# Summing half one's x1 + lam·y early on POOL, output stores on POOL's queue with more tiles, and the transform stored in loading order

## Chip, cores, metric

One core of one Trainium2 chip. Times are device microseconds of one execution on that core. "Engine" means PE (matrix multiply), DVE (vector), ACT (activation), POOL (GpSimd) or SP, which here does nothing but issue transfers: all the loads, so that I call its queue the loading queue, and some stores. A "queue" is the series of transfers that one of these engines issues, in its own program order. All runs in this text are of the fast state, with a mean granted PE clock between 0.907 and 0.925.

## The reference, cut to what matters

Two layers on an image of 256 channels of 256x128. The change touches only the end of the second. In the reference:

```python
attn = instance_norm(attn + tokens, attn_norm_w, attn_norm_b)
attn = attn.reshape(b * (C // TOKEN_CODIM), TOKEN_CODIM, H, W)
h0 = instance_norm(attn, norm2_w, norm2_b)
h1 = fno_layer(h0, mix_wr[0], ..., (H, W), norm=True, act=True)   # Gelu
h2 = fno_layer(h1, mix_wr[1], ..., (H, W), norm=True)
out = instance_norm(h2, mon_w, mon_b) + attn
# and around it:  x = x + layer(_gn(x))
```

In the kernel's names: `x1` is the image after layer one, `y` the attention output before its norm, `lam` a factor per channel. The last line is, per pixel, `x1 + lam*y + kap*h2 + c0`. `x1 + lam*y` does not depend on h1 or h2, so it can be had as soon as `lam` is known. The 256 channels are two halves (a = 0, 1) of 128 partitions; a half is 16 blocks of 2048 pixels (NB), 1 MB each in f32.

## The kernel before

```python
# stage A: y of both halves, 16 blocks each
    ...
    nc.scalar.dma_start(ydv[:, a, b * NB : (b + 1) * NB], yt)
# stage B: first_modes, end
    for a, h in enumerate(halves):
        synth_modes(wp, pss, Z[:, :, :, a * P : (a + 1) * P], P, h.Gd1, f"g1{a}", turned=True)

def first_images(a, beside=None):
    def begin(b):
        if a == 0 and b >= 4:
            yt = hb[b]                      # y is still in SBUF
        else:
            yt = wp.tile([P, NB], FP, tag="yt", ...)
            nc.sync.dma_start(yt, ydv[:, a, b * NB : (b + 1) * NB])
        ...                                 # PE: skip and image into ps
        for j in range(4):
            nc.scalar.activation(by_turn(hb[b])[:, j], ps[j]..., AF.Gelu)
    for b in range(17):
        if b < 16:
            if beside is not None:
                beside(b, op, psk)          # second_images(0, b)
            begin(b)
        if b > 0:
            ...                             # transposes hT, statistics, psA of block b - 1
            nc.scalar.copy(yA, psA)
            nc.scalar.dma_start(h.Yd[:, b - 1, :], yA)

def second_modes(a):
    ...   # YT <- Yd: sixteen loads; norm z; synthesis g2a

def second_images(a, b, wp, psk):
    for s in range(2):
        yt.append(wp.tile([P, half], FP, tag="yo", ..., bufs=2))
        nc.sync.dma_start(yt[s], ydv[:, a, px])
        xt.append(wp.tile([P, half], FP, tag="xo", ..., bufs=3))
        nc.sync.dma_start(xt[s], x1v[:, a, px])
    ...                                     # PE, then ACT Identity into hb[b]
    for s in range(2):
        nc.vector.scalar_tensor_tensor(xt[s], yt[s], lam, xt[s], ALU.mult, ALU.add)
        nc.vector.tensor_tensor(xt[s], xt[s], hb[b][...], ALU.add)
        nc.scalar.dma_start(outv[:, a, px], xt[s])

first_modes()                                            # B
first_images(0)                                          # C
second_modes(0)                                          # D
first_images(1, beside=... second_images(0, b, ...))     # E
second_modes(1)                                          # F
for b in range(16): second_images(1, b, wp, psk)         # G
```

`yA` (128x512) is the transform of one block. The pace of the yA copies is the pace of the blocks, and it serves as the clock of stages C and E in everything below.

## Time and profile before

3370.2 us median of four runs (3364.2 to 3379.4); the profiled run's span is 3364.9 us. The prediction names seven stages, A to G, and shows a table of them with rounded borders. For exact lengths I take as borders instructions that the loading queue issues in every variant: the first y load of C, the load of the transform that begins D and F, the first x or y load of E and G. B is counted from 2479.4 us, where A ends in before. A's last addition ends somewhat later in most other runs (2480.2 us in after, 2488.6 at the latest), and this difference, which belongs to what comes before B, is then in B's length too.

| stage | what it does | us | bound, as the prediction reads it |
|---|---|---|---|
| B | first modes, both halves | 103.7 | serial |
| C | first images of half one | 141.5 | PE |
| D | second modes of half one | 76.4 | serial |
| E | first images of half two, second images of half one | 285.8 | transfers |
| F | second modes of half two | 77.1 | serial |
| G | second images of half two | 201.0 | transfers and tiles |

Two more views matter later. The first is ACT's timeline of before in C: start, duration, instruction, and in brackets the idle time ahead of it and what ended it.

```profile
2627.68 0.58 ACT L1221 COPY yA<-psA 128x512 f32<-128x512 f32 x1 [3.25 <-PE psA L1217]
...
2629.82 2.06 ACT L1168 ACTIVATE blocks<-ups 128x512 f32<-128x512 f32 x4 [1.56 <-PE ups L949]
2631.74 0.62 ACT L1181 COPY hT<-htps 128x512 f32<-128x512 f32 x1
2635.61 0.58 ACT L1221 COPY yA<-psA 128x512 f32<-128x512 f32 x1 [3.25 <-PE psA L1217]
```

One block takes 2635.61 - 2627.68 = 7.93 us. ACT works 0.58 + 2.06 + 0.62 us of it and otherwise waits for PE. There is room for more on ACT, provided it stands in ACT's order where the gaps are.

The second is the loading queue's own waits in E (total us, times, longest).

```profile
SPq L1306 <- DMA out_dram<-x: 84.5, 27, 7.3
SPq L1304 <- DVE x L1319: 35.0, 21, 3.0
```

The queue stands 120 of E's 286 us for xo and yo tiles to come free.

### The profile page before, as it was taken

The page shows a single profiled execution, that of the slowest core. Times are in us where ns is not written, and L with a number is a line of the kernel's source. Part 1 is how long each engine was busy: PE and PEld are TensorE (multiplying, and loading weights), DVE is VectorE, ACT ScalarE, POOL GpSimd, SP SyncE. Part 2 cuts the span into 40 slices and gives each one's busy share as a digit, 9 for nine tenths or more (in the row PEclk, how much of TensorE's full clock was granted, in tenths as well). Part 3 has the DMA queues.
Part 4 walks back from the last instruction along what each step waited for, and adds up shares of the span by engine and source line. Part 5 has one row for each costly group of instructions (what it writes and reads, how often), then busy time and mean ns, then how long its engine had stood idle before and what let it go on. Part 6 is the DMA issues. An engine that isn't in the chain of part 4 may idle for free. (4 is left out here: it accounts for less than half of the span.)

```text
span 3364.9 us, 71699 instructions
## 1 busy us (share of the span) xinstructions
PE 2926.9 (87%) x30059; PEld 1956.8 (58%) x30059; DVE 1910.7 (57%) x2873; ACT 1231.2 (37%) x2266; POOL 1002.3 (30%) x807
## 2 busy tenths in 40 slices
PE   7799999999999999999996884989976966775765
PEld 6577777777777777777774473744434434332443
DVE  8566666666666666666666115746662534554433
ACT  0355555555555555555553101000002312332122
POOL 0255555555555555555553002000000000000000
PEclk9899999999999999999998966999988987898855
DMA  9222212211222112221220000188725237986487
GB/s 374 96 62 62 61 60 63 62 61 61 61 63 63 60 62 61 63 62 59 61 62 18 0 19 1 51 289 293 289 105 169 66 70 261 307 314 172 156 282 263
DMA packets 237101, 400.64 MB, mean 119 GB/s; under 512 B 23622, under 2 KB 181785, under 8 KB 221673
## 3 DMA queue, kind: packets, MB, share of 16 engines
q1 hardware_dynamic: 209896, 316.33, 29.1%
q10 hardware_dynamic: 26880, 79.70, 6.4%
q8 instruction: 238, 3.90, 0.5%
q14 instruction: 87, 0.70, 0.1%
HBM read 260.68 MB, written 135.27 MB: 118 GB/s over the span
## 5 line engine op out<-in xcount | busy, mean ns | idle before, releaser
L263 POOL TENSOR_TENSOR e<-e,b1T 128x1024 f32<-128x1024 f32 x256 | 609.5, 2381 | 103.6 <-ACT e L261 103.4
L282 DVE RECIPROCAL rd<-av 128x256 f32<-128x256 f32 x256 | 448.3, 1751 | 0.0
L284 POOL TENSOR_TENSOR og<-t,rd 128x256 f32<-128x256 f32 x256 | 185.8, 726 | 612.0 <-PE sc L253 593.8
L312 ACT COPY U<-u 128x129 f32<-128x129 f32 x256 | 99.3, 388 | 718.7 <-DVE stats L311 718.7
L281 DVE SCALAR_TENSOR_TENSOR t<-gate,av 128x256 f32<-128x256 f32 x256 | 107.9, 422 | 400.8 <-ACT gate L244 383.2
L262 DVE TENSOR_TENSOR e<-sc,b1T 128x1024 f32<-128x1024 f32 x256 | 309.0, 1207 | 2.5 <-PE sc L253 2.5
L253 PE MATMUL sc<-qkT 32*128 32x256 f32 x4096 | 293.4, 400 | 0.1
L264 ACT ACTIVATE e<-e 128x1024 f32<-128x1024 f32 x256 | 276.1, 1079 | 0.6 <-DVE e L262 0.4
L275 PE MATMUL av<-e,v 128*32 128x256 f32 x4096 | 274.7, 385 | 0.5 <-POOL e L263 0.5
L261 ACT ACTIVATE e<-sc 128x1024 f32<-128x1024 f32 x256 | 271.4, 1060 | 3.9 <-PE sc L253 3.7
L275 PE MATMUL av<-e,eb 128*32 128x256 f32 x4096 | 268.2, 379 | 0.0
L1025 PE MATMUL yps<-xt,mpT 128*128 128x512 f32 x512 | 230.2, 603 | 13.2 <-DMA xt<-x1d 13.2
L287 POOL TENSOR_TENSOR xb<-xt,bo 128x256 f32<-128x256 f32 x256 | 186.6, 729 | 120.5 <-DMA kt<-in_L_conv_kv_x_dram 120.5
L240 DVE TENSOR_TENSOR v<-gv,eb 128x256 f32<-128x256 f32 x256 | 108.8, 425 | 197.5 <-PE gv L237 197.3
L253 PEld LDWEIGHTS sc<-qkT 32*128 32x128 f32 x4096 | 185.3, 184 | 37.2 <-ACT qkT L230 0.8
L293 PEld LDWEIGHTS wo<-wo_half,og 128*128 128x128 f32 x1024 | 133.5, 190 | 106.9 <-issue 104.1
L275 PEld LDWEIGHTS av<-e,eb 128*32 128x32 f32 x4096 | 133.5, 110 | 87.7
L293 PE MATMUL wo<-wo_half,og 128*128 128x128 f32 x1024 | 182.2, 301 | 1.9 <-POOL og L284 1.9
L275 PEld LDWEIGHTS av<-e,v 128*32 128x32 f32 x4096 | 107.1, 109 | 129.5 <-ACT xnT L219 80.7
L1319 DVE SCALAR_TENSOR_TENSOR x<-y,col,x 128x1024 f32<-128x1024 f32 x64 | 82.2, 1284 | 175.9 <-DMA x<-x1d 163.8
L1025 PEld LDWEIGHTS yps<-xt,mpT 128*128 128x128 f32 x512 | 95.6, 192 | 125.1 <-issue 113.3
L233 PEld LDWEIGHTS gv<-wT_wv,kvT 128*128 128x128 f32 x1024 | 154.7, 191 | 13.1
(585 smaller groups left out, 5279.3 us busy)
## 6 DMA issues: line engine op xcount, KB each, us to landing
xb<-in_x_dram SPq DMA_DIRECT2D x32, 1024.0 KB
xt<-in_x_dram SPq DMA_DIRECT2D x128, 256.0 KB
kt<-in_L_conv_kv_x_dram SPq DMA_DIRECT2D x128, 256.0 KB
x1d<-x SPq DMA_DIRECT2D x256, 128.0 KB
xt<-x1d SPq DMA_DIRECT2D x32, 1024.0 KB
y<-yd SPq DMA_DIRECT2D x64, 512.0 KB
x<-x1d SPq DMA_DIRECT2D x64, 512.0 KB
out_dram<-x ACTq DMA_DIRECT2D x64, 512.0 KB
```

Of the source, the lines that this page charges most:

```text
L233: nc.tensor.matmul(ps[:, 256 + c * P : 256 + (c + 1) * P], kvT[:, c * P : (c + 1) * P], wT["wv"], start=True, stop=True,)
L253: nc.tensor.matmul(sc[h // 2][:, h % 2, c * 256 : (c + 1) * 256], qkT[p, 256 + c * P : 256 + (c + 1) * P], qkT[p, 0:256], start=True, stop ...
L261: nc.scalar.activation(e[1], s1[1], AF.Exp)
L262: nc.vector.tensor_tensor(e[0], s1[0], b1[0], ALU.add)
L263: nc.gpsimd.tensor_tensor(e[1], e[1], b1[1], ALU.mult)
L264: nc.scalar.activation(e[0], e[0], AF.Exp)
L275: nc.tensor.matmul(ps[hd, den * 256 : (den + 1) * 256], w, r["e"][h // 2][:, h % 2, c, :], start=(c == 0), stop=(c == 1),)
L282: nc.vector.reciprocal(rd, ps[:, 256:512])
L284: nc.gpsimd.tensor_tensor(r["og"], t, rd, ALU.mult)
L287: nc.gpsimd.tensor_tensor(r["xb"], r["x"], bc(bo, 1, 2), ALU.add)
L293: nc.tensor.matmul(ps[:, j * P : (j + 1) * P], r["og"][:, j * P : (j + 1) * P], wo, start=True, stop=True)
L1025: nc.tensor.matmul(ps[j].rearrange("p (n w) -> p n w", w=W), mpT[:, sc, tt], by_turn(xt[:, sc])[:, j], start=(sc == 0), stop=False,)
```

## The change

Its intent is to relieve E, where transfers bind, by work in C, where POOL and the DMA engines have room, and to give the output stages more room in flight. In parts:

1. **Sum.** For twelve of half one's sixteen blocks, C computes `wd = x1 + lam*y` (scale on ACT, add on POOL, store on POOL's queue). E loads `wd` instead of x1 and y. Those twelve y blocks are no longer stored in A. The other four are all loaded ahead of C's first modes.
2. **Queue and tiles.** Output stores are issued by POOL instead of ACT; four xo and two yo tiles in E (before three and two), eight and four in G.
3. **Transform order.** The transform is stored as four small transfers per block on the loading queue, and loaded in eight transfers of long runs (before sixteen, alternating between two queues).
4. **Synthesis moved.** Half two's first synthesis g11 goes from B to D; g10, which stays, gets eight PSUM buffers for four.
5. **Norm.** Its sum is taken by columns and used again for a second sum. No run below undoes this part.

```diff
 # A
-                    nc.scalar.dma_start(ydv[:, a, b * NB : (b + 1) * NB], yt)
+                    if a or b < 4:
+                        nc.scalar.dma_start(ydv[:, a, b * NB : (b + 1) * NB], yt)
 # B
-                        for a, h in enumerate(halves):
-                            synth_modes(..., h.Gd1, f"g1{a}", turned=True)
+                        nc.sync.dma_start(Z1d..., Z[:, :, :, P:]...)
+                        synth_modes(..., halves[0].Gd1, "g10", turned=True, banks=8)
 # C
+                if a == 0:
+                    for b in range(4):
+                        nc.sync.dma_start(hb[b], ydv[:, a, b * NB : (b + 1) * NB])
                     def begin(b):
-                        if a == 0 and b >= 4:
+                        if a == 0:
                             yt = hb[b]
+                            if b >= 4:
+                                for s in range(2):
+                                    px = slice(s * NB // 2, (s + 1) * NB // 2)
+                                    xt = wp.tile([P, NB // 2], FP, tag="xw", ..., bufs=3)
+                                    nc.sync.dma_start(xt, x1v[:, a, ...])
+                                    wt = wp.tile([P, NB // 2], FP, tag="ww", ..., bufs=3)
+                                    nc.scalar.activation(wt, yt[:, px], AF.Identity, scale=lam)
+                                    nc.gpsimd.tensor_tensor(wt, wt, xt, ALU.add)
+                                    nc.gpsimd.dma_start(wd[:, b - 4, px], wt)
...
-                            nc.scalar.dma_start(h.Yd[:, b - 1, :], yA)
+                            for j in range(4):
+                                nc.sync.dma_start(h.Yd[j, b - 1]..., yA[32 * j : 32 * j + 32, :]...)
 # D
-                                for r in range(2):
-                                    (nc.sync if r else nc.scalar).dma_start(YT[..., hc, r], h.Yd[...])
+                                nc.sync.dma_start(YT[32 * j : 32 * j + 32, hc]..., h.Yd[j, 8 * hc : 8 * hc + 8]...)
...
                         synth_modes(gp, psum, Z, P, h.Gd2, f"g2{a}")
+                        if a == 0:
+                            Z1 = gp.tile([P, 4, 2, P], FP, name="Z1", bufs=1)
+                            nc.sync.dma_start(Z1, Z1d)
+                            synth_modes(gp, psum, Z1, P, halves[1].Gd1, "g11", turned=True)
 # E and G
+                added = a == 0 and b >= 4
+                    if added:
+                        nc.sync.dma_start(xt[s], wd[:, b - 4, ...])
+                        continue
...
-                    nc.scalar.dma_start(outv[:, a, px], xt[s])
+                    nc.gpsimd.dma_start(outv[:, a, px], xt[s])
```

(Cut: the norm, and the tile counts, which are (3, 2) before and become (4, 2) in E and (8, 4) in G.)

More of the change, by code (lines that the diff above doesn't have):

```diff
@@ L473, in layer1, with synth_modes @@
         Fyd = dram.tile([P, 4, 2, NT], FP, name="Fyd")
-        def synth_modes(pool, psum, Z, T, Gd, tag, spare=None, turned=False):
+        def synth_modes(pool, psum, Z, T, Gd, tag, spare=None, turned=False, banks=4):
             both = 512 // T == 4
@@ L481, in synth_modes @@
                 for part in range(1 if both else 2):
-                    ps = [psum.tile([P, 512], FP, tag="s", name=f"{tag}gp_{c}_{part}_{f}", bufs=4) for f in range(4)]
+                    ps = [psum.tile([P, 512], FP, tag="s", name=f"{tag}gp_{c}_{part}_{f}", bufs=banks) for f in range(4)]
                     gt = pool.tile([P, 4, 512], FP, tag="gt", name=f"{tag}gt_{c}_{part}", bufs=2)
@@ L1072, in mix_modes @@
                     nc.scalar.activation(sq[:, r], by_c[r], AF.Square)
-                ps = psum.tile([P, 512], FP, tag="a", name=tag + "ens")
-                for c in range(4):
-                    for r in range(2):
-                        nc.tensor.matmul(
-                            ps[:, 0:T], om0[:, min(c, 1), :], sq[:, r, c, :],
-                            start=(c == 0 and r == 0), stop=(c == 3 and r == 1),
-                        )
-                en = wp.tile([P, T], FP, tag="en", name=tag + "en", bufs=1)
@@ L1081, in mix_modes @@
-                nc.vector.tensor_copy(en, ps[:, 0:T])
-                rs = wp.tile([P, T], FP, tag="rs", name=tag + "rs", bufs=1)
-                rsqrt(nc, wp, rs, en, EPS, "rs")
+                en = psum.tile([P, 512], FP, tag="a", name=tag + "ens", bufs=2)
+                for k in range(nh):
+                    for c in range(4):
+                        for r in range(2):
+                            nc.tensor.matmul(
+                                en[:, k : k + 1], sq[:, r, c, k * P : (k + 1) * P], om0[:, min(c, 1), 0:1],
+                                start=(c == 0 and r == 0), stop=(c == 3 and r == 1),
+                            )
@@ new lines, in mix_modes @@
+                rs = wp.tile([P, 2, nh], FP, tag="rs", name=tag + "rs", bufs=1)
+                rsqrt(nc, wp, rs[:, 0, :], en[:, 0:nh], EPS, "rs")
+                left = rs[:, 1, :]
+                nc.vector.tensor_mul(left, rs[:, 0, :], rs[:, 0, :])
+                nc.vector.tensor_mul(left, left, en[:, 0:nh])
+                dg = wp.tile([P, nh, P], FP, tag="dgz", name=tag + "dg", bufs=1)
+                for k in range(nh):
+                    nc.vector.tensor_scalar(dg[:, k, :], ident, rs[:, 0, k : k + 1], None, ALU.mult)
@@ L1084, in mix_modes @@
+                ps = psum.tile([P, 512], FP, tag="a", name=tag + "rsp", bufs=2)
+                nc.tensor.matmul(ps[:, 0:T], ones, dg.rearrange("p k t -> p (k t)"), start=True, stop=True)
+                rsb = wp.tile([P, T], FP, tag="rsb", name=tag + "rsb", bufs=1)
+                nc.scalar.copy(rsb, ps[:, 0:T])
                 Z = wp.tile([P, 4, 2, T], FP, tag="Z", name=tag + "Z", bufs=1)
                 for r in range(2):
-                    nc.vector.tensor_tensor(Z[:, :, r, :], by_c[r], bc(rs, 1, 4), ALU.mult)
+                    nc.vector.tensor_tensor(Z[:, :, r, :], by_c[r], bc(rsb, 1, 4), ALU.mult)
@@ L1087, in mix_modes @@
                 nc.vector.memset(Z[0:1, 0, 0, :], 0.0)
-                return Z, sq
+                return Z, left
             class Half:
@@ L1100, in layer1 @@
                 h.Gd2 = dram.tile([32, 4, 64, P], FP, name=f"Gd2_{a}")
-                h.Yd = dram.tile([P, 16, 512], FP, name=f"Yd_{a}")
+                h.Yd = dram.tile([4, 16, 4, 32, P], FP, name=f"Yd_{a}")
+            Z1d = dram.tile([P, 4, 2, P], FP, name="Z1d")
+            wd = dram.tile([P, 12, NB], FP, name="wd")
             def first_modes():
@@ L1123, in first_modes @@
                         nc.vector.tensor_scalar(h.bl0, blk[0], rho, None, ALU.mult)
-                    ps = psum.tile([P, 512], FP, tag="a", name="rhops")
+                    ps = psum.tile([P, 512], FP, tag="a", name="rhops", bufs=2)
                     nc.tensor.matmul(ps, ones, dg.rearrange("p k a t -> p (k a t)"), start=True, stop=True)
@@ L1142, in first_modes @@
                     with tc.tile_pool(name="mp0s", bufs=1, space=PSUM) as pss:
-                        for a, h in enumerate(halves):
-                            synth_modes(wp, pss, Z[:, :, :, a * P : (a + 1) * P], P, h.Gd1, f"g1{a}", turned=True)
+                        nc.sync.dma_start(
+                            Z1d.rearrange("p c r t -> p (c r) t"),
+                            Z[:, :, :, P:].rearrange("p c r t -> p (c r) t"),
+                        )
+                        synth_modes(wp, pss, Z[:, :, :, 0:P], P, halves[0].Gd1, "g10", turned=True, banks=8)
             def first_images(a, beside=None):
                 h = halves[a]
+                lam = h.col[:, 3:4]
+                if a == 0:
+                    for b in range(4):
+                        nc.sync.dma_start(hb[b], ydv[:, a, b * NB : (b + 1) * NB])
                 with tc.tile_pool(name="hp", bufs=2) as wp, tc.tile_pool(
@@ L1156, in begin @@
                     def begin(b):
-                        if a == 0 and b >= 4:
+                        if a == 0:
                             yt = hb[b]
+                            if b >= 4:
+                                for s in range(2):
+                                    px = slice(s * NB // 2, (s + 1) * NB // 2)
+                                    xt = wp.tile([P, NB // 2], FP, tag="xw", name=f"xw_{b}_{s}", bufs=3)
+                                    nc.sync.dma_start(xt, x1v[:, a, b * NB + px.start : b * NB + px.stop])
+                                    wt = wp.tile([P, NB // 2], FP, tag="ww", name=f"ww_{b}_{s}", bufs=3)
+                                    nc.scalar.activation(wt, yt[:, px], AF.Identity, scale=lam)
+                                    nc.gpsimd.tensor_tensor(wt, wt, xt, ALU.add)
+                                    nc.gpsimd.dma_start(wd[:, b - 4, px], wt)
                         else:
@@ L1221, in first_images @@
                             nc.scalar.copy(yA, psA)
-                            nc.scalar.dma_start(h.Yd[:, b - 1, :], yA)
+                            for j in range(4):
+                                nc.sync.dma_start(
+                                    h.Yd[j, b - 1].rearrange("n f t -> f n t"),
+                                    yA[32 * j : 32 * j + 32, :].rearrange("f (n t) -> f n t", n=4),
+                                )
             def second_modes(a):
@@ L1236, in second_modes @@
                             for j in range(4):
-                                for r in range(2):
-                                    (nc.sync if r else nc.scalar).dma_start(
-                                        YT[32 * j : 32 * j + 32, hc, r],
-                                        h.Yd[32 * j + 16 * r : 32 * j + 16 * r + 16, 8 * hc : 8 * hc + 8, :].rearrange(
-                                            "f b (n t) -> (b n) f t", n=4
-                                        ),
-                                    )
+                                nc.sync.dma_start(
+                                    YT[32 * j : 32 * j + 32, hc].rearrange("p r f t -> p (r f t)"),
+                                    h.Yd[j, 8 * hc : 8 * hc + 8].rearrange("b n f t -> (b n) (f t)"),
+                                )
                         for c in range(4):
@@ L1256, in second_modes @@
                             nc.vector.tensor_copy(F[:, c].rearrange("p r t -> p (r t)"), ps[:, 0:256])
-                    Z, sq = mix_modes(wp, psum, F, 1, P, f"z{a}")
+                    Z, left = mix_modes(wp, psum, F, 1, P, f"z{a}")
                     with tc.tile_pool(name="gtp", bufs=2) as gp:
                         synth_modes(gp, psum, Z, P, h.Gd2, f"g2{a}")
+                        if a == 0:
+                            Z1 = gp.tile([P, 4, 2, P], FP, name="Z1", bufs=1)
+                            nc.sync.dma_start(Z1, Z1d)
+                            synth_modes(gp, psum, Z1, P, halves[1].Gd1, "g11", turned=True)
                     Fw = wp.tile([P, 2, P], FP, tag="Fw", name=f"Fw_{a}", bufs=1)
@@ L1275, in second_modes @@
                     nc.vector.scalar_tensor_tensor(hv, ps[:, 0:1], 4.0, hv, ALU.mult, ALU.add)
-                    ps = psum.tile([P, 512], FP, tag="a", name=f"lfps_{a}")
-                    for c in range(4):
-                        for r in range(2):
-                            nc.tensor.matmul(
-                                ps[:, 0:1], sq[:, r, c, :], om0[:, min(c, 1), 0:1],
-                                start=(c == 0 and r == 0), stop=(c == 3 and r == 1),
-                            )
-                    nc.vector.tensor_scalar(r2, ps[:, 0:1], EPS, None, ALU.add)
-                    nc.vector.reciprocal(r2, r2)
-                    nc.vector.scalar_tensor_tensor(hv, ps[:, 0:1], r2, hv, ALU.mult, ALU.add)
+                    nc.vector.tensor_add(hv, hv, left)
                     rsqrt(nc, cp, kap, hv, EPS, "c3")
@@ L1293, in second_modes, with second_images @@
                     nc.vector.tensor_sub(c0, c0, r2)
-            def second_images(a, b, wp, psk):
+            def second_images(a, b, wp, psk, bufs):
                 h = halves[a]
@@ L1302, in second_images @@
                     px = slice(b * NB + s * half, b * NB + (s + 1) * half)
-                    yt.append(wp.tile([P, half], FP, tag="yo", name=f"y4_{a}_{b}_{s}", bufs=2))
+                    xt.append(wp.tile([P, half], FP, tag="xo", name=f"x4_{a}_{b}_{s}", bufs=bufs[0]))
+                    if added:
+                        nc.sync.dma_start(xt[s], wd[:, b - 4, s * half : (s + 1) * half])
+                        continue
+                    nc.sync.dma_start(xt[s], x1v[:, a, px])
+                    yt.append(wp.tile([P, half], FP, tag="yo", name=f"y4_{a}_{b}_{s}", bufs=bufs[1]))
                     nc.sync.dma_start(yt[s], ydv[:, a, px])
-                    xt.append(wp.tile([P, half], FP, tag="xo", name=f"x4_{a}_{b}_{s}", bufs=3))
-                    nc.sync.dma_start(xt[s], x1v[:, a, px])
                 gs = wp.tile([P, 4, P], FP, tag="gs3", name=f"gs3_{a}_{b}", bufs=2)
@@ L1318, in second_images @@
                     px = slice(b * NB + s * half, b * NB + (s + 1) * half)
-                    nc.vector.scalar_tensor_tensor(xt[s], yt[s], lam, xt[s], ALU.mult, ALU.add)
+                    if not added:
+                        nc.vector.scalar_tensor_tensor(xt[s], yt[s], lam, xt[s], ALU.mult, ALU.add)
                     nc.vector.tensor_tensor(xt[s], xt[s], hb[b][:, s * half : (s + 1) * half], ALU.add)
-                    nc.scalar.dma_start(outv[:, a, px], xt[s])
+                    nc.gpsimd.dma_start(outv[:, a, px], xt[s])
             first_modes()
@@ L1329, in layer1 @@
             second_modes(0)
-            first_images(1, beside=lambda b, wp, psk: second_images(0, b, wp, psk))
+            first_images(1, beside=lambda b, wp, psk: second_images(0, b, wp, psk, (4, 2)))
             second_modes(1)
@@ L1333, in layer1 @@
                 for b in range(16):
-                    second_images(1, b, wp, psk)
+                    second_images(1, b, wp, psk, (8, 4))
 def constants():
```

## The prediction

> **What bounds the kernel now.** I first read the busy shares by 40 slices on the page, to find the stages, then the chain of waits in order of time for their exact borders, then one table of busy times for the seven stages that the change touches. Everything before 2206 us is the first layer and the attention and is not touched.
>
> ```profile
> core 0: us, PE busy (x) PEld busy (x) DVE busy (x) ACT busy (x) POOL busy (x), PEclk, DMA share, GB/s
> 2206.00:2479.00 273.00, 263.31 (x1536) 127.06 (x1536) 155.82 (x252) 0.00 (x0) 0.00 (x0) 0.98 0.77 277
> 2479.00:2583.00 104.00, 64.50 (x1114) 40.39 (x1114) 51.62 (x98) 12.93 (x24) 0.00 (x0) 0.78 0.30 92
> 2583.00:2722.00 139.00, 122.71 (x1920) 57.38 (x1920) 72.12 (x113) 51.16 (x97) 0.00 (x0) 0.96 0.27 91
> 2722.00:2801.00 79.00, 44.79 (x626) 32.98 (x626) 25.87 (x54) 7.56 (x14) 0.00 (x0) 0.78 0.52 110
> 2801.00:3086.00 285.00, 213.55 (x2928) 91.57 (x2912) 152.55 (x181) 95.97 (x161) 0.00 (x0) 0.88 0.81 281
> 3086.00:3166.00 80.00, 46.94 (x651) 34.57 (x658) 24.86 (x57) 7.28 (x13) 0.00 (x0) 0.77 0.52 111
> 3166.00:3365.00 199.00, 119.56 (x991) 74.45 (x960) 77.64 (x64) 47.36 (x64) 0.00 (x0) 0.58 0.79 273
> ```
>
> Call the rows A (y = attention output, with its stores), B (modes of both halves), C (first images of half one), D (second modes of half one), E (first images of half two beside second images of half one), F (second modes of half two), G (second images of half two). A and C have PE near full and a full clock: they are PE's. C uses little DMA (share 0.27), POOL not at all. E and G have DMA shares of 0.81 and 0.79 and slow clocks: transfers set them. B, D and F are serial passages with idle gaps on everything.
>
> What kind of transfer bound G is, the waits of the loading queue over that stage tell:
>
> ```profile
> SPq L1306 <- DMA out_dram<-x: 77.9, 27, 7.5
> SPq L1304 <- DVE x L1319: 48.1, 19, 4.2
> ```
>
> The loading queue stood 77.9 us for an output store to give back an xo tile and 48.1 us for a yo tile: not only bandwidth but tiles. The chain of waits shows the round, about 12.6 us per block:
>
> ```profile
> 3248.51 6.46 DMA out_dram<-x
> 3255.02 3.42 DMA x<-x1d
> 3261.02 6.60 DMA out_dram<-x
> 3267.70 3.54 DMA x<-x1d
> ```
>
> A store of 512 KB (two are sent at once) took about 6.5 us to come back, a load 3.4 to 3.5 us. In E the same two waits are 84.5 and 35.0 us. The full rate of the transfer engines I take from rows of the same trace: 273/0.79 = 346, 281/0.81 = 347 GB/s; I use 345.
>
> The costs of the new work on ACT and POOL come from two groups with the same shape in the first layer:
>
> ```profile
> L263 POOL TENSOR_TENSOR e<-e,b1T 128x1024 f32<-128x1024 f32 x256 | 609.5, 2381 | 103.6 <-ACT e L261 103.4
> L264 ACT ACTIVATE e<-e 128x1024 f32<-128x1024 f32 x256 | 276.1, 1079 | 0.6 <-DVE e L262 0.4
> ```
>
> **What the Trainium skill says.** (1) "DMA: Bandwidth & Descriptors", section "Issuing engines are not separate DMA queues": queues of different engines end on the same 16 DMA engines, so moving stores to POOL saves queue time, no bandwidth. No run here shows it yet; the trace of before has no POOL transfer. (2) The same page, "SWDGE vs HWDGE vs iDMA": POOL's transfers have their descriptors written by POOL's own cores. Their first byte comes after about 1 us against 0.6. I estimate 1 us of POOL per store from this; not shown here. (3) "SBUF — State Buffer", "Door 1: The DMA port swizzle": 32 partitions reach only 8 of 16 ports, about 218 GB/s at most. The trace agrees: loading the transform, 32 partitions at a time, ran at 162 GB/s with the DMA share at 1.01 (2724 to 2750). (4) The same page, "SBUF: two separate sides": POOL and DVE block each other where DVE runs a two-port mode or reads two SBUF inputs. In C, DVE only copies and counts from PSUM, so I add nothing to POOL's 2.38 us.
>
> **The change part by part.**
>
> *A.* Twelve stores of 1 MB of y go. A is PE's, and its last store stays. Zero.
>
> *B.* The synthesis for half two leaves. B's two halves of it ran from 2542.5 to 2583; the last store of the first landed about 2563.5, that of the second at 2583. Both are paced by 4.2 MB of stores (252 GB/s in 2560 to 2583). Minus 18, plus 2 for a new 0.5 MB store of Z: **-16**. The norm by columns instead of by rows takes away 128x256 reciprocals (1.75 us) and adds a matmul and a copy: zero.
>
> *D.* That synthesis comes back here. The new order of PE's instructions has it after the g20 synthesis and before the last cv products and the first second image, and its 16 stores stand ahead of the next loads in the loading queue. So all of it is on the path: **+16**. The second sum over the squares goes (16 matmuls, 2.37 us), since the norm's own sum is used again: -2. The transform load took 2724.6 to 2749.3, 24.7 us for 4.2 MB; in loading order it has 8 transfers of 16 KB runs, but still 32 partitions each. At about 200 GB/s it takes 21: **-4**. D: +10.
>
> *F.* The same without the synthesis: -4 - 2 = **-6**.
>
> *C.* Here I expect a cost. It receives 24 half tiles: a load of x1 (512 KB), an ACT scale (1.08), a POOL add (2.38), a store (512 KB). Summed over the 139 us all fit: POOL 24 x 3.4 = 82, ACT 51 + 26 = 77, DMA 12.6 (0.27 share already there) + 25.2 MB. But the order of instructions, which can be had without running, does not spread them: all 24 scales stand in ACT's order before the copy of the fifth yA (end of the fifth block of sixteen), mixed with the Gelus, which PE needs. ACT takes its instructions in order, and a scale needs a free ww tile, of which there are three. One turn of a tile: 1.1 scale + 2.4 add + 1 descriptors + 5.5 to 6.5 store + hand-overs 0.4 = 10.4 to 11.4, so 3.5 to 3.8 us per half tile; POOL alone would need 3.4. The first add can start about 18 us into C: four y loads of 1 MB (12 us) now stand ahead of the first modes, and the second x1 load waits for the first image. So the last scale comes at about 18 + 21 x 3.6 + 2 = 96 us, and the fifth yA at 97. Before, yA copies came every 7.94 us and the fifth at 2635.6 or 53 us into C. The remaining eleven blocks run at PE's pace. **+45** (97 - 53 = 44, and 1 for the slower clock).
>
> *E.* Twelve of sixteen blocks load one summed tile instead of x1 and y: -12.6 MB of 79.7; the transform stores now have runs of 512 B instead of 2 KB, which I set at +10 us of engine time. DMA time: 0.81 x 285 = 231, minus 12.6 MB / 0.345 = 36, plus 10: 205. The other bound is the compute round: yA copies came 13.0 us apart at the quickest (2997.01 to 3010.60 and 3030.4 to 3043.3 show 13.0 to 13.6), on average 16.6 us (2844.94 to 3077.34 in 14 steps). DVE loses 2.6 us per summed block, ACT no longer holds output stores in its queue (28.4 us of Gelu waits behind DVE's x). I take 16.5 for three blocks and 13.9 for eleven: 14 steps = 202 instead of 232, so -30; and about -12 from the filling and the first blocks, with four xo tiles for three. **-42.**
>
> *G.* 54.5 MB at 345 GB/s are 158 us; at 95% 166, plus about 5 for the first modes and the last tile's way out. 199 - 171 = **-28**, if eight and four tiles let the loads run two blocks ahead.
>
> Sum: -16 + 45 + 10 - 42 - 6 - 28 = **-37**; 3373.5 - 37 = **3336.5**.
>
> **Rivals.** *C stays PE's*: the scheduler's mixture does not bind because POOL and the store are quicker than I think (turn of 8 us): ACT's waits disappear in the Gelu gaps, C costs only +10. For it: the sums over the whole stage fit. Against it: the order is fixed, and 24 x 2.38 alone are 57 us for a stretch that took 53. Total about 3300. *C becomes worse*: x1 loads wait behind yA stores on the one loading queue, and 25 MB collide with the rest; a turn of 14 us, C +75, total about 3366. *E and G are short of bandwidth, not of tiles*: more tiles only lengthen the queue (the store takes 8 instead of 6.5 us), E -20, G -10; total about 3377. For it: one of the 40 slices, in E, already reaches 314 GB/s. Against it: the loading queue stands still for 126 of G's 199 us. *POOL's stores lag*: each output store starts 1 us later and nothing else; with four tiles, harmless.
>
> **Range and chances.** C is uncertain by about 25 us, E and G together by about 30, B and D by 8: together about 40, a range of about plus or minus 55. Faster by over 2% needs 3306 or less: a cheap C with full gains in E and G. Slower by over 2% needs 3441: almost every step would have to fail. I shade to the quicker side, since the gains in E and G rest on measured waits and the loss in C on an estimate of POOL's store: the time 3336, range 3275 to 3390.
>
> **What would show it right or wrong.** In the profile after: C about 180 us long, PE's share there below 75%, ACT's scales waiting for stores of ww, POOL busy 57 us or more, the pace of yA slow for five blocks, then 7.9 us; B shorter by 16 and D longer by about 10; transform load 20 to 22 us; yA every 14 us in E; G near 171 at a DMA share of 0.9 and the loading queue's wait for output stores under 25 us. I am wrong if C stays under 155 us or passes 205, if D's added synthesis hides behind its transfers, or if G keeps its 12.6 us per block.

## The result, and the profile after

After: 3338.95 us median of four fast runs (3337.75 to 3339.36). The ratio is 0.9904, 95% interval 0.988 to 0.9929: quicker by 1%, within 2%, 3 us from the predicted time. (Predicted was a gain of 37 us on 3373.5; the medians differ by 31, the profiled spans by 27.) Ratios here and below are the mean time of one kernel's fast runs over that of the other's fast runs of the same rounds, so not quite the ratio of the medians quoted.

The table by stage of the kernel after, with exact borders, rows B to G (columns as in the prediction's table: borders, length, busy time with instruction counts of PE, PE's weight loads, DVE, ACT and POOL, then granted clock, DMA share, GB/s):

```profile
2479.40:2565.26 85.86, 50.35 (x620) 29.07 (x620) 44.51 (x96) 8.79 (x17) 0.00 (x0) 0.73 0.22 68
2565.26:2760.47 195.21, 133.63 (x1920) 61.93 (x1920) 74.62 (x113) 77.55 (x121) 69.95 (x48) 0.84 0.59 195
2760.47:2853.22 92.75, 58.03 (x1124) 44.20 (x1124) 28.51 (x63) 11.74 (x22) 0.00 (x0) 0.78 0.54 143
2853.22:3100.31 247.09, 196.51 (x2912) 83.89 (x2912) 122.23 (x153) 96.03 (x161) 17.06 (x32) 0.93 0.80 274
3100.31:3178.93 78.62, 46.71 (x644) 35.01 (x644) 23.16 (x55) 7.45 (x14) 0.00 (x0) 0.75 0.44 108
3178.93:3337.50 158.57, 101.98 (x960) 64.54 (x960) 76.84 (x64) 46.79 (x64) 17.05 (x32) 0.62 0.94 345
```

| stage | before | after | difference | predicted |
|---|---|---|---|---|
| B | 103.7 | 85.9 | -17.8 | -16 |
| C | 141.5 | 195.2 | **+53.7** | +45 |
| D | 76.4 | 92.8 | +16.4 | +10 |
| E | 285.8 | 247.1 | **-38.7** | -42 |
| F | 77.1 | 78.6 | +1.5 | -6 |
| G | 201.0 | 158.6 | **-42.4** | -28 |
| sum | | | -27.3 | -37 |

The sum is the difference of the two profiled spans. Gains of 99 us and losses of 72 us stand behind a change of 27.

**C after.** ACT's timeline around the last scale (ww):

```profile
2661.10 2.39 ACT L1186 ACTIVATE ww<-blocks,col 128x1024 f32<-128x1024 f32 x2 [0.97 <-DMA wd<-ww]
...
2669.72 1.15 ACT L1186 ACTIVATE ww<-blocks,col 128x1024 f32<-128x1024 f32 x1 [3.81 <-DMA wd<-ww]
2670.78 0.57 ACT L1251 COPY yA<-psA 128x512 f32<-128x512 f32 x1
...
2678.46 0.59 ACT L1251 COPY yA<-psA 128x512 f32<-128x512 f32 x1 [3.25 <-PE psA L1247]
...
2686.39 0.59 ACT L1251 COPY yA<-psA 128x512 f32<-128x512 f32 x1 [3.25 <-PE psA L1247]
```

The last scale waits for a store of an earlier ww tile to land, and the fifth yA copy comes right behind it, at 2670.8 or 105.5 us into C (before: 52.5). From there on the pace is 7.9 us as before. The row for the stretch up to this copy:

```profile
2565.26:2670.78 105.52, 53.57 (x680) 24.74 (x696) 23.33 (x35) 44.51 (x59) 67.03 (x46) 0.70 0.87 303
```

PE is busy for half of it; POOL for 67 us, and the DMA engines have a share of 0.87. ACT's waits in C and POOL's groups there (count | busy us, mean ns):

```profile
ACT ww L1186 <- DMA wd<-ww: 39.4, 15, 10.2
ACT yA L1251 <- PE psA L1247: 38.9, 12, 5.3
```

```profile
L1187 POOL TENSOR_TENSOR ww<-ww,xw 128x1024 f32<-128x1024 f32 x24 | 56.4, 2351 | 493.1 <-DMA xw<-x1d 482.3 <-ACT ww L1186 10.4 <-ACT hT L1211 0.3
L1188 POOL DMA_DIRECT2D wd<-ww x24 | 13.8, 574 | 4.8 <-POOL ww L1187 4.2 <-DMA xw<-x1d 0.3 <-DMA wd<-ww 0.3
```

An add takes 2.35 us and issuing a store occupies POOL for 0.57 us. (The 482 us idle is the time since POOL's last work in the first layer.) The adds start 18.0 us into C and come 3.81 us apart.

**E after.** ACT's timeline in the middle of E:

```profile
3010.43 0.59 ACT L1251 COPY yA<-psA 128x512 f32<-128x512 f32 x1 [3.25 <-PE psA L1247]
3012.57 2.79 ACT L1342 ACTIVATE blocks<-h2ps,col 128x512 f32<-128x512 f32 x4 [1.55 <-PE h2ps L949]
3017.87 2.06 ACT L1198 ACTIVATE blocks<-ups 128x512 f32<-128x512 f32 x4 [2.51 <-DVE x L1350]
3019.79 0.62 ACT L1211 COPY hT<-htps 128x512 f32<-128x512 f32 x1
3023.66 0.59 ACT L1251 COPY yA<-psA 128x512 f32<-128x512 f32 x1 [3.25 <-PE psA L1247]
```

The round is 13.23 us, and it is this long for twelve blocks in a row: PE, ACT, DVE, ACT, PE, none of them waiting for a transfer. The 2.51 us ahead of the Gelu (L1198) is part of the round: the Gelu of half two overwrites `hb[b]`, which DVE must first have added to half one's output.

**G after.** The loading queue's waits:

```profile
SPq L1335 <- DMA y<-yd: 44.3, 30, 2.3
SPq L1333 <- DMA x<-x1d: 32.4, 19, 2.2
```

The 126 us of waiting for tiles are gone. What is left is waiting for the queue's own earlier loads, and the stage moves 345 GB/s at a DMA share of 0.94: now bandwidth is nearly all of it. It is not quite the limit, since G of e1 and of e10 below moves 353 GB/s at 0.95.

**D.** The load of the transform, from issue (loading queue) to the matmul that needed all of it (PE):

```profile
2760.47 3.99 SPq L1271 DMA_DIRECT2D YT<-Yd  x8
```

```profile
2783.93 2.36 PE L1281 MATMUL f1ps<-YT,k_efwd 128*32 128x128 f32 x40 [7.37 <-DMA YT<-Yd]
```

23.5 us, against 24.6 before (2724.65 to 2749.29). From there to the g20 synthesis 30.4 (before 30.7), and from that to the first load of E 38.9 (before 21.1). Of these 17.8 us more the moved g11 is 15.6, since the step takes 23.3 in the run without the move (e6 below); the other 2.2 us are in F too (24.1, before 21.8).

### The profile page after: what moved, and what is told of

Its sections match the earlier page's. It is cut to its first block, busy times and chain, and to the rows that moved or that the text cites. A ratio compares the mean times of both kernels' runs of the same rounds, so it can differ in the third digit from the quotient of the medians.

```text
span 3337.5 us, 71936 instructions
## 1 busy us (share of the span) xinstructions
PE 2903.5 (87%) x30049; PEld 1942.7 (58%) x30049; DVE 1874.7 (56%) x2852; ACT 1258.2 (38%) x2293; POOL 1107.9 (33%) x919
## 3 DMA queue, kind: packets, MB, share of 16 engines
q1 hardware_dynamic: 221832, 329.97, 30.7%
## 5 line engine op out<-in xcount | busy, mean ns | idle before, releaser
L263 POOL TENSOR_TENSOR e<-e,b1T 128x1024 f32<-128x1024 f32 x256 | 609.8, 2382 | 103.7 <-ACT e L261 103.5
L1351 POOL DMA_DIRECT2D out_dram<-x x64 | 34.1, 533 | 621.1 <-DVE x L1350 314.6
L1187 POOL TENSOR_TENSOR ww<-ww,xw 128x1024 f32<-128x1024 f32 x24 | 56.4, 2351 | 493.1 <-DMA xw<-x1d 482.3
L1025 PEld LDWEIGHTS yps<-xt,mpT 128*128 128x128 f32 x512 | 95.4, 191 | 125.6 <-issue 113.6
```

Source lines behind the costliest of these rows:

```text
L263: nc.gpsimd.tensor_tensor(e[1], e[1], b1[1], ALU.mult)
L1025: nc.tensor.matmul(ps[j].rearrange("p (n w) -> p n w", w=W), mpT[:, sc, tt], by_turn(xt[:, sc])[:, j], start=(sc == 0), stop=False,)
```

## The experiments

Eleven kernels, three timed rounds each, all correct. The part or parts named are the only difference from the kernel that is named first. Stage lengths are read from the profiled run of each, with the same borders.

| run | us | ratio to before | B | C | D | E | F | G |
|---|---|---|---|---|---|---|---|---|
| e1_no_sum | 3330.8 | 0.9876 | 87.6 | 148.2 | 82.6 | 300.3 | 76.6 | 155.0 |
| e2_act_queue | 3361.9 | 0.9972 | 85.7 | 197.8 | 93.5 | 263.0 | 76.4 | 165.4 |
| e3_few_tiles | 3380.2 | 1.0032 | 84.6 | 195.6 | 92.9 | 246.4 | 76.5 | 195.4 |
| e4_sum_alone | 3399.2 | 1.0069 | 110.2 | 195.6 | 78.2 | 262.2 | 76.4 | 200.4 |
| e5_old_order | 3343.9 | 0.9901 | 87.7 | 207.1 | 95.4 | 236.5 | 77.9 | 157.6 |
| e6_synth_back | 3338.2 | 0.9879 | 103.1 | 195.3 | 77.6 | 247.3 | 77.8 | 158.0 |
| e7_spread | 3295.5 | 0.9771 | 87.9 | 155.5 | 93.4 | 242.3 | 77.8 | 159.3 |
| e8_five_tiles | 3332.3 | 0.9869 | 90.2 | 191.5 | 94.3 | 243.2 | 78.0 | 156.7 |
| e9_spread_first | 3292.8 | 0.9755 | 88.5 | 154.0 | 93.7 | 243.0 | 77.9 | 157.5 |
| e10_no_sum_old_order | 3325.5 | 0.9857 | 86.6 | 150.8 | 83.7 | 288.0 | 78.2 | 154.8 |
| e11_spread_old_order | 3295.9 | 0.9753 | 94.4 | 153.4 | 94.3 | 237.9 | 80.0 | 157.9 |

The kernel before measured 3369.1 (e1 to e3, e7), 3371.0 (e4, e8 to e10) and 3377.2 us (e5, e6, e11) in the three sets of rounds, so the ratios compare better across calls than the medians do. A stage's length moves by 1 to 4 us between kernels that do the same in it (F, for instance, is 76.4 to 80.0). Column B carries what differs before B starts: counted from the end of A's last addition, B is 103.8 us in before, 105.9 in e4, 100.6 in e6, and 84.7 to 86.0 in after and all the others.

### e1: the change without the sum

```diff
-                            if b >= 4:        # the whole sum in begin(), and the guard of A's store
-                                ...
-                added = a == 0 and b >= 4
+                added = False
```

> The changed kernel with only the POOL sum undone (all 32 y stores back, second images load x1 and y again); tiles, POOL's stores, loading order and moved synthesis stay. Theory (the sum costs more in the first images of half one, C, than it saves in E): C falls from 195 to 145-150 us; E, which runs in a compute round of 13.23 us per block with the sum, goes back to transfers, 15 us per block for twelve blocks, about 265-272 us; total about 3310-3317, some 25 us BELOW the changed kernel. Rival (the sum is what made E quick, and C would be long anyway through its four leading y loads): E back to 285 or more, C 160 or more, total 3340 or more.

C came as expected (148.2), E did not: 300.3 instead of 265 to 272, which is the rival's side, and the total of 3331 missed the 3310 to 3317. ACT's wait and the loading queue's in E of e1:

```profile
ACT blocks L1188 <- DVE x L1340: 73.4, 14, 11.4
```

```profile
SPq L1323 <- DMA out_dram<-x: 69.0, 20, 6.2
SPq L1243 <- ACT yA L1241: 46.7, 7, 12.2
```

The Gelu waits 73.4 us for DVE (after: 35.1), and DVE waits for loads: the queue again stands for xo tiles, and now also for yA copies, whose stores are in it. So the sum is worth 53 us in E, and costs 47 in C and 10 in D; taken out of the finished change it gains 8 us by the medians, though the intervals of the two ratios overlap (0.9849 to 0.9903, and 0.9880 to 0.9929). My expectation failed because I took E's gain to come mostly from the rest of the change.

The 10 us in D have a cause of their own. In e1 the loading queue issues the first half of the transform during C, and only the second half at its end (2715.24, where I set the border):

```profile
2652.98 1.27 SPq L1261 DMA_DIRECT2D YT<-Yd  x1
...
2715.24 1.84 SPq L1261 DMA_DIRECT2D YT<-Yd  x4
```

All of it is there 13.1 us later (2728.32), not 23.5. In before and in after all loads of the transform stand behind C's end. That in after the ww and xw tiles hold the memory into which e1 loads early is likely, but no run tests it.

### e4: the sum alone, on the kernel before

```diff
 # kernel before, plus: wd, the sum in begin(), the store guard in A, and
+                added = a == 0 and b >= 4      # load wd into xo, no yo tile, no DVE multiply
```

> The kernel before with only the POOL sum added (twelve y stores gone, sums stored to and loaded from memory); stores on ACT's queue, three xo and two yo tiles, old transform order, both syntheses in the first modes. Theory (C pays about 50 us for 24 scales in ACT's first five blocks; E without twelve y loads comes near its compute round, but its output stores still share eight completion semaphores with the loads): C 185-195, E 255-265, G unchanged 200; total 3380-3395, slower than before by 15-25 us. Rival (the sum pays by itself): total below 3360.

Near its theory, a little worse than it: C is 195.6 (expected 185 to 195), so that the cost is the sum's own, to 0.4 us of after's. E gains 24 of the 39. The total of 3399 (expected 3380 to 3395) is slower than before by 0.7% (interval 0.4 to 1.0%).

### e2 and e3: the queue without the tiles, the tiles without the queue

```diff
 # e2
-                    nc.gpsimd.dma_start(outv[:, a, px], xt[s])
+                    nc.scalar.dma_start(outv[:, a, px], xt[s])
 # e3
-  second_images(0, b, wp, psk, (4, 2))     ...  second_images(1, b, wp, psk, (8, 4))
+  second_images(0, b, wp, psk, (3, 2))     ...  second_images(1, b, wp, psk, (3, 2))
```

> The changed kernel with only the output stores moved back to ACT's queue, tiles (4,2) and (8,4) kept. Theory (tiles made G quick, the queue little): G 158-163 us, E 247-255 us, total within 8 us of the changed kernel. Rival (the queue did it, since ACT no longer stands before stores that wait for DVE): E 265 or more, G 175 or more, total 3370 or more.

> The changed kernel with only the tiles of before (three xo, two yo in both stages), stores on POOL's queue. Theory (tiles): G back to 190-200 us, the loading queue waiting over 60 us for output stores there; E 250-260; total about 3375-3385. Rival (queue): G under 170 us, total 3340-3350.

e3 came as expected in G and in the total: G goes back to 195.4. E does not move (246.4, where 250 to 260 was expected). The fourth xo tile in E is worth nothing, the tiles in G 37 us. Its loading queue in G shows before's picture again:

```profile
SPq L1333 <- DMA out_dram<-x: 74.0, 29, 7.0
SPq L1335 <- DVE x L1349: 40.2, 21, 4.0
```

e2 missed: expected within 8 us of after, it is 23 us slower, 16 in E and 7 in G, between its theory and its rival. The loading queue in G of e2:

```profile
SPq L1333 <- DMA out_dram<-x: 24.3, 12, 3.7
SPq L1335 <- DMA y<-yd: 21.7, 14, 2.8
SPq L1333 <- DMA x<-x1d: 18.7, 13, 2.9
```

With eight xo tiles the loads still wait for output stores. The packed traces say why. They record for each transfer the semaphore on which its completion is counted, and what is waited for before it is issued. In e2 and in after all transfers of SP and of ACT complete on the same eight semaphores (numbers 100 to 106 and 109), all of POOL's on eight others (116 to 123), and a transfer waits for the one that used its semaphore before. Four of them in G, in my own layout:

```
e2:    3337.61 ACT  store out_dram<-x   completes on 106
       3342.77 SP   load  x<-x1d        waits for 106, whose last landing is at 3342.76
after: 3305.66 SP   load  x<-x1d        waits for 100 (SP's and ACT's) and 122 (POOL's)
       3318.76 POOL store out_dram<-x   completes on one of POOL's eight
```

The load at 3342.77 is the second x half of block 15, whose tile, of eight, block 11 had last; the store that it waits for is block 14's. In e2 a block's two output stores sit among its loads in one ring of eight, so some loads cannot be issued until a store has landed that has nothing to do with their tile. In after no output store is in that ring. The wait in the trace is shown; that the semaphore and not, say, ACT's order is all of the 23 us, is not separated: in E, ACT must also reach the store in its own order.

### e8: five ww and xw tiles instead of three

```diff
-  tag="xw", ..., bufs=3      tag="ww", ..., bufs=3
+  tag="xw", ..., bufs=5      tag="ww", ..., bufs=5
```

> The changed kernel with five ww and five xw tiles for three, order left to the scheduler. Theory (the ring of three tiles sets 3.8 us per half tile; with five, POOL's 2.35 + 0.57 + hand-overs of about 0.3 = 3.3 us sets it, or transfers at 3.4): C shorter by 8-14 us, 181-187; total about 3326-3331. Rival (transfers already saturate there): C stays 192-197, total as the changed kernel, 3336-3341.

C is 191.5, 3.7 less than in after; the ring theory had it at 181 to 187 and missed. So did the rival's 192 to 197, by less. The adds come 3.70 us apart instead of 3.81: more tiles do little, and the ring of three is not what sets this pace. What does is not settled; the stretch up to the fifth yA copy still has a DMA share of 0.85. That it holds up the blocks at all is a matter of order, as the next run shows.

### e7: the sums spread over twelve blocks

The scale of block b + 4 is put behind the start of block b, one per block, with a small copy of `lam` that is written late enough to keep the scheduler from moving the scale forward; four ww and xw tiles.

```diff
-                            if b >= 4: ...                       # sum out of begin()
+                    def summed(b):
+                        lamb = wp.tile([P, 1], FP, tag="lamb", ..., bufs=3)
+                        if b < 6:
+                            nc.vector.tensor_copy(lamb, lam)
+                        else:     # 0 * (a statistic of block b - 6) + lam
+                            nc.vector.tensor_scalar(lamb, hstat[:, 4 * (b - 6) + 3, 1:2], 0.0, lam, ALU.mult, ALU.add)
+                        ...       # the same sum, scale=lamb, 4 tiles of each kind
                             begin(b)
+                            if a == 0 and b < 12:
+                                summed(b + 4)
```

> The changed kernel with the sum kept but spread: the scale of block b+4 takes a factor that comes from the statistics of block b-2 (times zero, plus lam), so that ACT's order holds two scales per block over twelve blocks instead of all 24 in the first five; four ww and xw tiles. Theory (C is long because of the fixed order with a ring of three tiles at 3.8 us per half tile, not because of the work as such): C 148-160 us, E as in the changed kernel (247), total about 3295-3305. Rival (25 MB more in C collide with its own transfers and the work costs its time wherever it stands): C stays 180 or more, total 3325 or more.

C is 155.5 at the same work. Its row of the table:

```profile
2567.30:2722.80 155.50, 124.57 (x1920) 58.45 (x1920) 76.90 (x125) 76.31 (x121) 70.81 (x48) 0.93 0.74 245
```

ACT and POOL are as busy as in after (76 and 71 us), the DMA engines carry 245 instead of 195 GB/s, and ACT no longer waits for any store of ww. In the stretch in which e7 does its sums (2567.30 to 2680.50) the DMA engines even have a share of 0.92 at 312 GB/s, where after's lump had 0.87 at 303, and PE works beside it (88 of 113 us, in after 54 of 106). So C's 54 us were neither ACT's nor POOL's time nor bandwidth, but twelve blocks' sums standing in ACT's order ahead of the fifth block. (e7 has four tiles for three as well; by e8, with five, tiles are worth less than 4 us.) 0.9771 (0.9745 to 0.9797): faster than both.

### e9: the spread sums, and the first y loads in the order of need

```diff
-                    for b in range(4):
-                        nc.sync.dma_start(hb[b], ydv[...])
+                    nc.sync.dma_start(hb[0], ydv[:, a, 0:NB])    # hb[b + 1] after load_modes of block b
```

> The run with the sum spread, with only the first y tile loaded ahead of the first modes of C and the other three behind the modes, one per block. Theory (four y loads ahead of the modes cost C about 6 us at its start): C from 155.5 to 148-151, nothing else changes; total about 3288-3292. Rival (the later y tiles are then late themselves): C 154 or more.

C 154.0, total 3292.8, 0.9755: its C of 148 to 151 was missed, and the rival's number came. The total cannot be told from e7's. The four y loads ahead of the first modes cost at most 1.5 us once the sums are spread.

### e10, e5, e11: the transform's order

The old order is one store per block on ACT's queue and sixteen loads. e10 is e1 with it, e5 is after with it, e11 is e9 with it.

```diff
-                            for j in range(4):
-                                nc.sync.dma_start(h.Yd[j, b - 1]..., yA[32 * j : 32 * j + 32, :]...)
+                            nc.scalar.dma_start(h.Yd[:, b - 1, :], yA)
```

> The run without the sum, with the transform's storing and loading as before as well (one 256 KB store per block on ACT's queue for four of 64 KB on the loading queue). Theory (E took 300 us without the sum because each load waits for the eighth transfer before it on a shared set of eight completion semaphores, and four small stores per block that stand in the loading queue until yA is there take half of them): E falls from 300 to 265-278; F and D longer by 1-2 us; total about 3300-3312. Rival (E is simply limited by its 79.7 MB and two yo tiles): E 292 or more, total 3325 or more.

> The kernel after with the transform stored and loaded in its old order: one store per block on ACT's queue, sixteen loads of the transform. Theory (from the kernel after: issue to f1ps 23.4 us against 24.7 before): the loading order is worth 1 to 2 us in D and again in F and nothing else, so 3340 to 3344. Rival (from the two kernels without the sum, 3331 and 3326): the four small stores per block in the loading queue cost more in E than the loads gain, so 3327 to 3337, with E 243 or less.

> The best version so far (sums spread evenly over the first images, first y loads in need order, 3293) with the transform stored and loaded in its old order. In C ACT is now the engine with the order that binds, and the old order puts one store per block back on ACT's queue. If the loading queue is what is short in E (rival of the run without the sum): E 236 to 240 and 3285 to 3290. If the compute round of 13.2 us per block sets E: E 242 to 244, D and F 1 to 2 longer each, 3294 to 3298.

The small stores in the loading queue cost E 12 us without the sum (e1 to e10), 11 with it (after to e5), 5 with the spread sums (e9 to e11). E of e5 gains it mainly at the start: the first step between yA copies is 21.0 us in after and 13.2 in e5, since in after loads stand behind stores that wait for the first yA. D gets longer by 0.6 to 2.6 with the old order. In e5, C gets longer by 12 us, and the totals come out even: 0.9904 to 0.9901. They are even from e9 to e11 too (0.9755 to 0.9753), but there no stage of the change pays for E: e11's profiled run comes into A 6.4 us later than e9's (first matmul of A at 2222.8 and 2216.4), before anything that the change touches, and B to G together are 3 us shorter. Of e5 and e11 each side had one half right: E is shorter, as for those who count on the loading queue, and the total is no better, as for those who do not. e10's E of 288 missed the 265 to 278 and lies between the two sides; its total is the rival's. Why C takes 207 us in e5 I have not settled. All of the 12 us lie before the fifth yA copy, which comes 118.3 us into C (after: 105.5): the adds are 4.05 us apart (3.81), only one of the 24 scales is left behind the fourth yA copy (after: three), and the fifth comes 8.2 us after the last scale (after: 1.1). ACT's scales wait 52.0 us for ww stores (39.4 in after). It is not the old order as such, since e4 has it too and its C is 195.6.

### e6: the synthesis for half two back in B

```diff
-                        if a == 0:                           # in second_modes
-                            ... synth_modes(gp, psum, Z1, P, halves[1].Gd1, "g11", turned=True)
+                        for a, h in enumerate(halves):       # in first_modes, banks=8
+                            synth_modes(wp, pss, Z[:, :, :, a * P : (a + 1) * P], P, h.Gd1, f"g1{a}", turned=True, banks=8)
```

> The kernel after with the synthesis for half two back in the first modes. Theory: the move only carries 17 us from B to D, nothing hides in either place: B 102 to 105, D 74 to 77, total within 4 us of 3339. Rival: part of it hides beside the g20 synthesis in D, so bringing it back costs: B plus 17 but D minus 10 or less, 3345 or more.

As expected, D by 0.6 us outside. Rows B and D:

```profile
2479.40:2582.53 103.13, 59.44 (x1136) 37.19 (x1132) 51.39 (x106) 13.09 (x25) 0.00 (x0) 0.76 0.31 93
...
2777.79:2855.34 77.55, 45.52 (x612) 34.41 (x612) 23.24 (x55) 7.44 (x14) 0.00 (x0) 0.74 0.45 109
```

B +17.2, of which 1.8 us are A's later end, so 15.5 by itself; D -15.2; and the total cannot be told from after's (0.9879 and 0.9904, with overlapping intervals). The move carries some 15 us from one serial passage to another.

## Why the prediction was right

The time was right to 3 us, though the stages were off by up to 14, with both signs: that the total came so close is luck in part. Term by term:

- **C, +45 predicted, +53.7 measured.** That all 24 scales stand in ACT's order before the fifth yA copy is the mechanism predicted, and e7 shows it by taking it away. That the ring of three tiles sets the pace within the lump is not shown: e8's five tiles left 3.70 us. First add 18 us in (18.0), 3.5 to 3.8 us per half tile (3.81). The last scale was put at 96 us and came at 104. The term mis-sized is "21 x 3.6": the adds began on time and ran at the slow end of the range, 23 steps of 3.81 = 88 us. That POOL's store would take 1 us was an overestimate (0.57 us), and the stores landed in 5.7 us (median of 24), as put. From these numbers (1.15 + 2.35 + 0.57 + 5.7) I estimate a turn of about 10 us, or 3.3 per half tile; where the rest of the 3.81 comes from is open. The first rival, C stays PE's, is what e7 makes of it: C +14, total 3295, near its 3300.
- **G, -28 predicted, -42.4 measured.** The tiles are the main cause (e3: 37 of it), as the prediction read from the loading queue's waits. Two terms failed. The full rate of 345 GB/s, scaled from rows at a share near 0.8, was reached at 0.94, and passed in e1 (353), so the "95%" was subtracted from a limit that lies higher; and "about 5" for the first modes and the last tile's way out was no extra, since 54.7 MB at 345 GB/s are the whole 158.6 us. The queue's 7 us (e2) was set at nothing.
- **E, -42 predicted, -38.7 measured, for partly wrong reasons.** The pace, 13.9 us predicted, is 13.2. But "about -12 from ... four xo tiles for three" is refuted: the fourth tile gives nothing (e3). POOL's queue gives 16 of the gain (e2), where the prediction had only ACT's 28.4 us of Gelu waits in view, and the small transform stores cost some 11 (e5). The sum is needed for all of it: without it, queue and tiles together leave E at 288 (e10), no better than before. Its own worth, 53 us (e1) or 52 with the old transform order (e10 to e5), exceeds the 36 us of transfer time that the prediction took for its 12.6 MB.
- **B and D.** -17.8 against -16, or -18.7 from A's end; the added synthesis on the path, 15.6 against +16 (e6), with 2.2 us more behind it in D that the prediction did not have. The synthesis gave B 15.5 (e6); the other 3 us are what e6 has over before in B, where the norm and the PSUM buffers differ; the prediction had put the norm at zero. The step that failed is the transform load: -4 predicted at "about 200 GB/s", -1.2 measured, in D as in F (23.5 us for 24.7). Also failed: -2 for the second sum. It stood near the end of the stage, on PE's way to the second images (in before at 2796.3 to 2798.7), while the next stage's first load, where the border lies, waits for the synthesis's stores. In F, PE does come to the second images earlier, 73.1 us after F's start for 76.3; the first load does not.
- **F, -6 predicted, +1.5 measured**, from the same two failed terms and 2 us more between the synthesis and the first load.

In sum, of the errors C's 9 and D's and F's 14 were losses missed, G's 14 a gain missed, and E's 3 and B's 2 small; they leave 10 us in the difference of the profiled spans. The range of plus or minus 55 was fair to the stages; the sum needed far less of it, because their errors cancelled.

On what the prediction took from the Trainium skill: "DMA: Bandwidth & Descriptors", section "Issuing engines are not separate DMA queues", says that issuing from several engines saves only sequencer time. Here POOL's queue was worth 23 us (e2 against after); that its limit of bandwidth changed no run shows (G moved 331 GB/s at a share of 0.92 in e2, 345 at 0.94 in after). "SBUF — State Buffer", section "Door 1: The DMA port swizzle", gives about 218 GB/s at most for 32 partitions at a time, and the trace does not contradict it: the 4.2 MB went at 4.2/23.5 = 179 GB/s. But it does not explain the failed -4, since the predicted 200 lies under 218 as well and the share of the DMA engines in that load fell from 1.06 to 0.84; what holds the load is open. The same page, "SBUF: two separate sides": POOL's add in C took 2.35 us, as in the first layer (2.38), so there is no slowdown against it, as assumed.

## What to carry to other kernels

Work that fits an idle engine on average can still stop the busy one, if all of it stands in some engine's order ahead of what the busy one needs: count, in the instruction order, what comes before the fifth block, not what fits into the stage. Then spread it: the same work cost 54 us in a lump and 14 spread, which turned a change of 1% into one of 2.3%. When loads wait for stores, ask two questions apart, which tile is missing and which completion semaphore or queue they share; here the tiles were worth 37 us and the separate queue 23.

## What the Trainium skill lacked or had wrong

- "DMA: Bandwidth & Descriptors", "Issuing engines are not separate DMA queues": the page has that only the sequencer's time is saved; here more was. In this program SP's and ACT's transfers took turns on eight shared completion semaphores and POOL's had eight of their own; moving 64 output stores of 512 KB from ACT to POOL took 3361.9 to 3339.0 us, 16 us in E and 7 in G. How much of the 16 was ACT's own order is not separated.
- The same page: at its head it gives a first-byte latency of about 1 us for POOL's transfers, and its section "SWDGE vs HWDGE vs iDMA" says who writes the descriptors; neither says how long issuing one occupies POOL, which the prediction had to estimate. Here it took POOL 0.57 us for a store of 512 KB (24 in C, mean 574 ns), where the prediction had put 1 us.
- None of the pages cited here says how a busy share of the DMA engines is to be scaled to their limit. Rows at 0.79 to 0.81 with 272 to 281 GB/s, scaled to a share of 1, gave 345 GB/s; G then ran at 345 GB/s with a share of 0.94, and in e1 at 353 with 0.95.
